# The last image's tail in a two-layer scan kernel: the short scan in the slots' form, its norm and convolution input made inside the output pipeline

## The chip, the cores and the metric

The kernel runs on one core of a Trainium2 chip. The metric is the device time of one execution in microseconds. Five engines work from queues of their own: PE (matrix products into PSUM), DVE (vector work and scans), ACT (activation functions and copies), POOL (element-wise work in SBUF only) and SP (which here issues DMA transfers). They meet through semaphores.

## The reference

Eight images of 64 x 64 positions and 96 channels pass through two layers with residual connections. Each layer is

```python
x = x + layer(group_norm(x))       # 32 groups of 3 channels, over all positions
# layer:
xz = x @ in_proj                   # 96 -> 2 * 192 channels: a value and a gate z
v = silu(depthwise_conv3x3(value)) # 192 channels
y = sum of four scans over the 4096 positions (by rows, by columns, each both ways)
y = layernorm(y) * silu(z)
out = y @ out_proj                 # 192 -> 96
```

A scan of layer 0 is the usual selective scan, `h = exp(dt * A) * h + dt * B * u`, `y = sum over 16 states of h * C + D * u`, where dt (through a softplus), B and C come from the value by small projections. Layer 1 has one set of weights for the four directions, and its scan is written in closed form:

```python
decay = exp(cumsum(dt * A))                   # along the positions
h = decay * cumsum(dt * B * u / (decay + 1e-12))
y = sum over states of h * C + u * D
```

As the accumulated decay falls far below 1e-12, h goes to zero. So in layer 1 only the first positions of each direction add to y beyond u * D. The kernel computes 160 positions of each direction, and a flag computed on the chip (`worst`) tells whether that was enough; if not, a general path, not run here, redoes layer 1.

## The kernel before

**Layout.** Channels lie on partitions: 96 of them in each of NH = 2 halves, 4096 positions in the free dimension. A scan works on 128 partitions, which are 32 channels (a group; NG = 3 groups in a half) by 4 states; so a full tile needs NS = 4 *sets* to cover 16 states.

**The loop over images.** For each image b, `scan_rows` runs the scan of layer 0 in an order written out by hand (`manual_schedule`): step n issues, for neighbouring sets, the loads of replicated rows, the decay, the scan, the read-out and the summing products. Beside it, other stages placed at given steps compute the convolution of image b - 1's layer 1 and of image b + 1's layer 0. At the end of the scan of image b come the sets of the *short* scan of image b - 1's layer 1. Then `out_phase` runs the output pipeline of both finished maps: 8 chunks of 512 positions from each, 16 stages with fixed lags (load x, mean, centring, squares, variance, roots, scaling, affine, gate, projection, residual sum, store), and a plan by which other work can be put at chosen steps.

**The short scan in the slots' form**, as used for images 0 to 6. Only 160 positions at each of four starts matter, and states with larger rates die sooner: 160, 40, 24 and 16 positions suffice for the four sets of states (`HEADS`). All four sets and four directions are packed side by side into one row of 960 (`HT`) columns, so there is one set per group, six in all. `extend` makes the shorter copies of a row. `short_projection` makes dt's input, B and C; `short_ready` makes, per half (a *job*), softplus of dt (`parts`, `exponential`, `logarithm`, `rounded`, `rounding`, and `total`, which sums four terms by products with the identity), dt * u (`product`), the running sum of dt (`running`, `again`), the smallest products for the flag (`lowest`), and stores the three rows to DRAM (`store`). Its tiles dt0, z0, dtu0 and ln0 have one buffer each, and the running sum reuses dt0. Per set, `fetch` and `replicate_short` load the rows replicated over partitions, `fill` makes the decay, `drive` copies dt * u to PSUM, `gate` applies tanh to the running sum (the closed form's factor decay / (decay + 1e-12), written as half of 1 + tanh), and DVE does the rest:

```python
nc.vector.tensor_tensor(s["buf"], s["group"]["drive"], b, ALU.mult)
nc.vector.scalar_tensor_tensor(buf, s["group"]["cum"], 1.0, buf, ALU.add, ALU.mult)
for d in (slice(0, BLOCK), slice(HT - 1, BLOCK - 1, -1)):
    nc.vector.tensor_tensor_scan(
        buf[:, d], s["decay"][:, d], buf[:, d], 0.0, ALU.mult, ALU.add
    )
```

`read_out` multiplies by C on POOL and `collect` sums the states by products on PE. In the listings of profiles these are L857 (decay), L878 (drive), L872 (tanh), L895, L898 and L903 (DVE), L924 (POOL) and L937 (PE); L505 is the copy of `extend`, L798 that of `lowest`.

**The end** is `finish`, for image 7, which has no following image to run beside. In order: the output pipeline of image 7's layer 0 and image 6's layer 1; then the load of image 7's whole layer-0 output x1 from DRAM into the tile x1T (L1835) and of the convolution's weights (`late_conv`, L150 and L157; L159 multiplies the taps); the group norm from sums that the pipeline took; `conv_second`, which normalizes x1T into the padded map xn (L368) and runs `convolution`; then `scan_head`, a form of the short scan of its own; then the output pipeline of that map alone, and the flag.

`convolution` computes the first half's channels by PE up to row 40 and by ACT and POOL beyond it (L301, L303), the second half's by DVE from projections that PE makes and ACT copies into the padded maps xp (L255, L262, L290, L292), and ends each piece with a Silu on ACT (L294).

`scan_head` works on rows of 640 columns, 160 for each direction, for all states alike. POOL copies the starts (L1199), ACT multiplies the map by the summed D (L1238); rows are replicated over partitions by products with `spread` into PSUM (L1185). Each of the six groups does four sets of four scans on DVE (L1178), with a sigmoid for the factor (L1278), products on DVE and POOL (L1271, L1280, L1282) and the sums into the map (L1295). The order of this part, and of everything in `finish` outside of `out_phase`, follows the scheduler of the language from data dependences; tiles from pools that share memory wait for each other.

Of the kernel before, what the change touches and what calls it, by code (L numbers as in the profile page):

```python
# [17 lines left out]
NH = 2  # L18
# [20 lines left out]
CUTS = slice(0, MM), slice(MM, HN)  # L39
# [6 lines left out]

JOINS = slice(HEAD, 3 * HEAD, 2 * HEAD - 1)
# [6 lines left out]
def two_ss2d_layers(ctx: ExitStack, tc: tile.TileContext, t: dict, out: bass.AP):  # L54
# [300 lines left out]
    def conv_second(x1T, st, xc):  # L355

        rows = T // WW
        with (
            tc.tile_pool(name="conv", bufs=1) as pool,
            tc.tile_pool(name="pmm", bufs=4, space=PSUM) as pmm,  # L360
            tc.tile_pool(name="ptap", bufs=1, space=PSUM) as ptap,
        ):
            bank = lambda name: pmm.tile([P, MM], F32, tag="mm", name=name)
            late_conv(1, pool)
            gm, gr, shift = group_norm(st, bank)
            xn = padded(pool, "xn1")
            for i in range(NT):
                nc.vector.tensor_scalar(  # L368
                    xn[:, 1 + i * rows : 1 + (i + 1) * rows, 1 : 1 + WW],
                    grid(x1T[:, i * T : (i + 1) * T]),  # L370
                    gm,
                    gr,
                    ALU.subtract,
                    ALU.mult,
                )
            tap_bank = lambda name: ptap.tile([P, T], F32, name=name)
            convolution(1, xn, xc, pool, bank, tap_bank, PE_ROWS, rows)
        return gm, gr, shift
# [12 lines left out]
    def scan_parts(b):  # L391
# [20 lines left out]
        if b >= 1:  # L412
            unit = dict(short=True, nth=None, n=HT, b=b - 1)
            units.append(unit)
            for h in range(NH):
                jobs.append(dict(unit=unit, h=h))
                for g in range(NG):
                    group = dict(unit=unit, job=jobs[-1], h=h, g=g)
                    sets.append(dict(unit=unit, group=group, i=0, first=False))
        x_dbl = [dram.tile([2 * ROWS, L], F32, name=f"x_dbl{c}", bufs=2) for c in "rc"]  # L420
        return units, jobs, sets, x_dbl

# [83 lines left out]

    def fetch(s, short, loads):

        if s and s["i"] == 0 and s["unit"]["short"] == short:
            group, n = s["group"], s["unit"]["n"]  # L510
            for c in ("dt", "dtu", "cum") if short else ("dt", "dtu"):
                if c == "cum":
                    rep = loads.tile([P, T], F32, tag="bc_rep", name="cum_rep", bufs=2 * NS + 1)
# [17 lines left out]
    def replicate_short(s, c, loads):  # L531

        if s and s["unit"]["short"] and s["group"]["h"] == 0 and s["group"]["g"] == 0:
            unit = s["unit"]
            rep = loads.tile([P, T], F32, tag="bc_rep", name=f"{c}_rep", bufs=2 * NS + 1)
# [630 lines left out]
    def scan_head(xc, worst):  # L1166

        n, cuts, joins = HN, CUTS, JOINS

        def runs(out, decay, drive):

            for d in (slice(0, 2 * HEAD), slice(n - 1, 2 * HEAD - 1, -1)):
                nc.vector.tensor_tensor_scan(  # L1178
                    out[:, d], decay[:, d], drive[:, d], 0.0, ALU.mult, ALU.add
                )  # L1180

        def product(lhs, src, name, m=P):
            ps = psum.tile([P, T], F32, tag="ps", name=name)
            for at in cuts:
                nc.tensor.matmul(ps[:m, at], lhs, src[:, at], start=True, stop=True)  # L1185
            return ps[:m, :n]

        with tc.tile_pool(name="hpiece", bufs=1) as piece, tc.tile_pool(name="hwork", bufs=NS) as work:

            def spare(name, m=P):  # L1190
                bufs = 2 if name == "gate1" else NS
                return work.tile([P, n], F32, tag=name, name=name, bufs=bufs)[:m, :]

            load_late(piece, "spread")
            xs = [spare("decay1", C) for h in range(NH)]
            for h in range(NH):
                for k, at, src in segments(xc[:, h, :]):
                    dst = xs[h][:, k * HEAD + at.start : k * HEAD + at.stop]
                    nc.gpsimd.tensor_copy(shaped(dst, src), src)  # L1199
            m = R + 2 * N  # L1200
            ps = psum.tile([P, T], F32, tag="ps", name="ps_proj1")
            for at in cuts:
                for h in range(NH):
                    nc.tensor.matmul(
                        ps[:m, at],
                        w["wx1"][:, 0, h, :],
                        xs[h][:, at],
                        start=h == 0,
                        stop=h == NH - 1,
                    )  # L1210
            x_dbl = spare("gate1", m)
            nc.scalar.copy(x_dbl, ps[:m, :n])
            b_rep, c_rep = states_rep(x_dbl, n, piece)
            dt, dtu, cum = (
                piece.tile([C, NH, n], F32, name=f"h_{c}") for c in ("dt", "dtu", "cum")
            )
            z, ln = ([spare(c, C) for h in range(NH)] for c in ("drive1", "decay1"))
            for h in range(NH):
                bias = w["dtb1"][:, 0, h : h + 1]
                ps = product(w["dtw1"][:, 0, h * C : (h + 1) * C], x_dbl[:R, :], "ps_dt1", C)  # L1220
                nc.scalar.activation(dt[:, h, :], ps, AF.Relu, bias=bias)
                nc.scalar.activation(z[h], ps, AF.Abs, bias=bias)
            for h in range(NH):
                nc.scalar.activation(z[h], z[h], AF.Exp, scale=-1.0)
# [764 lines left out]
```

## Time and profile before

| quantity | us |
|---|---|
| median of three runs | 12404.24 (12389.48 to 12425.54) |
| the profiled execution, time | 12404.1 |
| its span | 12402.2 |
| output pipeline of two streams | 114.05 (from 11979.00) |
| gap before the convolution | 13.15 (from 12093.05) |
| convolution of layer 1 | 68.39 (from 12106.20) |
| `scan_head`, preparation | 27.06 (from 12174.59) |
| `scan_head`, six groups | 126.70 (from 12201.65) |
| last output pipeline | 69.25 (from 12328.35) |

The stages' borders are instructions in the timelines: the first PE or DVE work after a stage, the last sum of DVE before it. A row of a timeline gives start and length in us, the engine, the line of the kernel, the operation with its tiles, how many were merged, and in brackets how long the engine had idled and for whom. `PEclk` is the share of full rate that was granted to PE.

### The profile page before, as it was taken

Reading aid. Unit: us, or ns where it says so; the run is one execution under the profiler, and the core shown is the slowest. Engines: PE = TensorE matmul, PEld = TensorE weight load, DVE = VectorE, ACT = ScalarE, POOL = GpSimd, SP = SyncE. Lnnn points to the kernel's source line nnn. Section 1 sums busy time; section 2 is a strip of 40 time slices with the busy share of each in tenths; the row PEclk is TensorE's granted clock in tenths of the full one; section 3 lists DMA queues with packets and bytes.
Section 4 is the critical chain, followed back from the end, with each engine's and each line's share of the span. In section 5 each row is a group of like instructions: output and inputs, shape, how many; then the busy total and the mean of one; then the engine's idle time right before and its main releaser. Section 6 shows DMA issues by size and latency. Waiting matters only on the chain. (4 is left out here: it accounts for less than half of the span.)

```text
span 12402.2 us, 134216 instructions
## 1 busy us (share of the span) xinstructions
PE 9540.3 (77%) x44312; PEld 3022.4 (24%) x44312; DVE 10960.4 (88%) x6870; ACT 9688.3 (78%) x15131; POOL 10508.3 (85%) x4802
## 2 busy tenths in 40 slices
PE   5875578787888778877788777888788887886565
PEld 1221122222222222222222222222222222222122
DVE  6999889996999969999799987999879998899976
ACT  4888778887887868878788787887778877788874
POOL 3999889996999969998699986999879987799974
PEclk8887778888888878888888878887788877887786
DMA  3444344444444444444444454444544445444430
GB/s 96 165 155 156 127 159 161 154 156 152 148 164 160 161 138 164 163 162 147 148 156 158 162 165 135 160 162 161 163 138 153 156 156 158 136 165 160 157 123 23
DMA packets 666561, 1853.80 MB, mean 149 GB/s; under 512 B 184936, under 2 KB 199150, under 8 KB 665757
## 3 DMA queue, kind: packets, MB, share of 16 engines
q1 hardware_dynamic: 658685, 1832.52, 44.6%
q10 hardware_dynamic: 7168, 12.59, 0.3%
q8 instruction: 352, 5.77, 0.2%
q14 instruction: 356, 2.92, 0.1%
HBM read 1533.82 MB, written 311.02 MB: 149 GB/s over the span
## 5 line engine op out<-in xcount | busy, mean ns | idle before, releaser
L924 POOL TENSOR_TENSOR out<-set,c_rep 128x1024 f32<-128x1024 f32 x3114 | 7290.0, 2359 | 884.4 <-PE acc L960 317.8
L908 DVE TENSOR_TENSOR_SCAN set<-decay,state,set 128x1024 f32<-128x1024 f32 x2304 | 5366.3, 2345 | 407.4 <-ACT decay L861 189.6
L861 ACT ACTIVATE decay<-dt_rep,w_a 128x1024 f32<-128x1024 f32 x3072 | 3420.2, 1114 | 335.7 <-DVE set L908 329.8
L895 DVE TENSOR_TENSOR set<-drive,b_rep 128x1024 f32<-128x1024 f32 x2346 | 2811.1, 1198 | 43.1 <-DMA b_rep<-x_dblr 28.2
L1027 PE MATMUL ps_conv<-edged,taps 96*96 96x512 f32 (+1 forms) x4032 | 2476.3, 754 | 54.5 <-DVE dt L787 25.9
L960 PE MATMUL acc<-out,w_gather 128*32 128x256 f32 x24576 | 2274.2, 480 | 8.1 <-POOL out L924 7.7
L908 DVE TENSOR_TENSOR_SCAN set<-decay,set 128x1024 f32<-128x1024 f32 x768 | 1744.4, 2286 | 224.5 <-ACT decay L861 146.6
L885 POOL TENSOR_TENSOR set<-dtu_rep,b_rep 128x1024 f32<-128x1024 f32 x768 | 1810.1, 2357 | 93.9 <-DMA b_rep<-x_dblr 51.6
L951 PE MATMUL acc<-map,w_eye 96*32 96x256 f32 x4608 | 568.5, 575 | 1483.4 <-ACT map L990 1253.5
L990 ACT COPY map<-acc 32x256 f32<-32x256 f32 x3072 | 1470.5, 479 | 45.8 <-PE acc L960 5.6
L960 PEld LDWEIGHTS acc<-out,w_gather 128*32 128x32 f32 x24576 | 781.8, 130 | 1939.5 <-issue 1282.0
L1027 PEld LDWEIGHTS ps_conv<-edged,taps 96*96 96x96 f32 (+1 forms) x4032 | 727.5, 200 | 1405.4 <-issue 1244.3
L919 ACT COPY state<-set 128x1 f32<-128x1 f32 x2304 | 426.1, 185 | 754.3 <-DVE set L908 747.9
L634 PE MATMUL ps_sp<-z,w_eye 96*96 96x512 f32 x960 | 658.2, 774 | 288.8 <-ACT ln L643 244.4
L655 POOL TENSOR_TENSOR dtu<-ln,map 96x1024 f32<-96x1024 f32 x256 | 670.7, 2620 | 237.2 <-DVE ln L651 133.0
L878 ACT COPY drive<-dtu_rep 128x1024 f32<-128x1024 f32 (+1 forms) x810 | 808.0, 997 | 34.7 <-DMA dtu_rep<-dtu_far 30.1
L602 PE MATMUL ps_dt<-x_dbl,w_dtw 7*96 7x512 f32 x1024 | 595.4, 663 | 301.2 <-ACT z L615 151.0
L951 PEld LDWEIGHTS acc<-map,w_eye 96*32 96x32 f32 x4608 | 101.4, 121 | 1954.6 <-ACT map L990 1656.1
L634 PE MATMUL ps_sp<-dtu,w_eye 96*96 96x512 f32 x960 | 554.6, 662 | 0.0
L634 PE MATMUL ps_sp<-ln,w_eye 96*96 96x512 f32 x960 | 535.5, 642 | 0.0
L614 ACT ACTIVATE dt<-ps_dt 96x512 f32<-96x512 f32 x512 | 303.0, 592 | 279.2 <-PE ps_dt L602 260.0
L634 PE MATMUL ps_sp<-dt,w_eye 96*96 96x512 f32 x960 | 506.7, 610 | 0.0
(239 smaller groups left out, 9496.8 us busy)
## 6 DMA issues: line engine op xcount, KB each, us to landing
dt_rep<-dt_far SPq DMA_DIRECT2D x768, 512.0 KB
dtu_rep<-dtu_far SPq DMA_DIRECT2D x768, 512.0 KB
b_rep<-x_dblr SPq DMA_DIRECT2D x256, 512.0 KB
c_rep<-x_dblr SPq DMA_DIRECT2D x256, 512.0 KB
b_rep<-x_dblc SPq DMA_DIRECT2D x256, 512.0 KB
c_rep<-x_dblc SPq DMA_DIRECT2D x256, 512.0 KB
dt_far<-ln SPq DMA_DIRECT2D x256, 384.0 KB
dtu_far<-dtu SPq DMA_DIRECT2D x256, 384.0 KB
```

The costliest lines, as they stand in the source:

```text
L634: nc.tensor.matmul(job["ps"][:C, :], w["eye"], job[term][:, halves[s]], start=i == 0, stop=i == 3,)
L655: nc.gpsimd.tensor_tensor(like(job["dtu"], col), like(job["dt"], col), positions(xc[:, h, :], col, t0, T), ALU.mult,)
L861: nc.scalar.activation(s["decay"], s["group"]["dt"], AF.Exp, scale=rate)
L878: nc.scalar.copy(s["group"]["drive"], s["group"]["dtu"])
L885: nc.gpsimd.tensor_tensor(s["buf"], s["group"]["dtu"], b, ALU.mult)
L895: nc.vector.tensor_tensor(s["buf"], s["group"]["drive"], b, ALU.mult)
L908: nc.vector.tensor_tensor_scan(ordered(s["buf"], unit), ordered(s["decay"], unit), ordered(s["buf"], unit), 0.0 if unit["nth"] == 0 else s ...
L924: nc.gpsimd.tensor_tensor(s["out"], s["buf"], s["unit"]["c", s["i"]], ALU.mult)
L951: nc.tensor.matmul(acc, lhs[:, GC * g : GC * (g + 1)], positions(old[:, h, :], unit["column"], unit["t0"] + at, n), start=True, stop=False ...
L960: nc.tensor.matmul(acc, w["gather"], s["out"][:, at : at + n], start=False, stop=s["i"] == NS - 1, skip_group_check=True,)
L990: nc.scalar.copy(yk, like(acc, unit["column"]))
L1027: nc.tensor.matmul(job["ps"][:C, :], taps[l][:k, h, tap, :], edged[:k, tap // 3 : tap // 3 + rows, tap % 3 : tap % 3 + WW], start=tap == 0 ...
```

## The change

Four things change, all in what follows the scan of image 7.

1. `finish` lets the output pipeline keep the new x in x1T: chunks of x are loaded straight into slices of x1T and the residual sum is written there. It is still stored to DRAM, but no longer loaded back. x1T and a pool `last` with xn and the convolution's weights are allocated on the right side, where the scan's loads were.
2. The group norm's stages are put at steps 19 to 24 of that output pipeline, with one load of ACT's table ahead of the last, and the four pieces of normalization (`stage_second`) at steps 26 to 29. `late_conv` runs before the pipeline.
3. The map of image 6 in that pipeline (y1) takes a buffer of `keep` under the tag "map".
4. `scan_head` and its constants are gone. `scan_last` uses the slots' form: the twelve copies of starts on DVE, `extend`, `short_projection`, `short_ready` for both jobs, the products by the summed D on DVE, then a loop in hand-written order over the six sets. `add_sums` adds each group's sums into the map. The ring of replicated rows has 4 buffers instead of 9.

```diff
+    def stage_second(x1T, xn, i, norm):
+        rows = T // WW
+        at = xn[:, 1 + i * rows : 1 + (i + 1) * rows, 1 : 1 + WW]
+        src = grid(x1T[:, i * T : (i + 1) * T])
+        nc.vector.tensor_scalar(at, src, norm[0], norm[1], ALU.subtract, ALU.mult)

-    def conv_second(x1T, st, xc):
+    def conv_second(x1T, st, xc, staged=None):
...
-            late_conv(1, pool)
-            gm, gr, shift = group_norm(st, bank)
-            xn = padded(pool, "xn1")
...
+            if staged:
+                xn, norm = staged
+            else:
+                late_conv(1, pool)
+                norm = group_norm(st, bank)
+                xn = padded(pool, "xn1")
+                for i in range(NT):
+                    stage_second(x1T, xn, i, norm)

-                    rep = loads.tile([P, T], F32, tag="bc_rep", name="cum_rep", bufs=2 * NS + 1)
+                    rep = loads.tile([P, T], F32, tag="bc_rep", name="cum_rep", bufs=ring(s))

-    def scan_head(xc, worst):
...
+    def scan_last(b, xc):
+        unit, jobs, sets = short_parts(b)
+        unit["ring"] = 4
+        with (
+            tc.tile_pool(name="piece", bufs=1) as piece,
+            tc.tile_pool(name="loads", bufs=2) as loads,
+            tc.tile_pool(name="work", bufs=2) as work,
+        ):
+            xs[b] = piece.tile([C, NH, HT], F32, name="x_short")
+            for h in range(NH):
+                for k, at, src in segments(xc[:, h, :]):
+                    dst = xs[b][:, h, place(0, k)][:, at]
+                    nc.vector.tensor_copy(shaped(dst, src), src)
+                extend(xs[b][:, h, :])
+            with tc.tile_pool(name="pmisc", bufs=4, space=PSUM) as pmisc:
+                for _, stage in short_projection(xc, None, unit, piece, pmisc):
+                    stage()
+                for job in jobs:
+                    for _, stage in short_ready(xc, None, job, piece, pmisc):
+                        stage()
                 for h in range(NH):
...
+                    for i in range(NT):
+                        at = xc[:, h, i * T : (i + 1) * T]
+                        nc.vector.tensor_scalar(
+                            at, at, w["dsum1"][:, h : h + 1], None, ALU.mult
+                        )
...
+                for n in range(-4, len(sets) + 4):
+                    at = lambda i: sets[n + i] if 0 <= n + i < len(sets) else None
+                    replicate_short(at(AHEAD_BC), "b", loads)
+                    fetch(at(2), True, loads)
+                    replicate_short(at(AHEAD_BC - 1), "c", loads)
+                    advance_set(at(0), None, work)
+                    fill(at(1), pslot)
+                    drive(at(1), True, pdrive)
+                    gate(at(1))
+                    read_out(at(-1), work)
+                    collect(at(-2), xc, xc, pacc)
+                    add_sums(at(-3), xc)
+
+    def add_sums(s, y):
+        if not s:
+            return
+        h, g = s["group"]["h"], s["group"]["g"]
+        for k, at, dst in segments(y[GC * g : GC * (g + 1), h, :]):
+            part = shaped(s["group"]["acc"][GC * k : GC * (k + 1), at], dst)
+            nc.vector.scalar_tensor_tensor(dst, part, 0.5, dst, ALU.mult, ALU.add)

     def finish(b, y):
...
-        with tc.tile_pool(name="x1T", bufs=1) as pool1:
+        with tc.tile_pool(name="x1T", bufs=1, side="right") as pool1:
             x1T = pool1.tile([C, L], F32, name="x1T")
-            nc.sync.dma_start(x1T, x1[b])
-            xc = keep.tile([C, NH, L], F32, name="map")
-            norm = conv_second(x1T, st, xc)
-            with rotating():
-                scan_head(xc, worst)
+            with tc.tile_pool(name="last", bufs=1, side="right") as last:
+                late_conv(1, last)
+                xn = padded(last, "xn1")
+                with tc.tile_pool(name="behind", bufs=1) as pool:
+                    plan, put = planner()
+                    def chunk(i, _):
+                        x = x1T[:, i * MM : (i + 1) * MM]
+                        nc.sync.dma_start(x, t["x"][b][:, i * MM : (i + 1) * MM])
+                        return x
+                    first = list(finish_first(b, y, st, pool))
+                    first[3] = chunk
+                    streams = [tuple(first)]
+                    if b >= 1:
+                        streams.append(second_of(b - 1, keep, pool, pool, put))
+                    def beside(pmm):
+                        bank = lambda name: pmm.tile([P, MM], F32, tag="mm", name=name)
+                        stages, found[1] = group_norm_stages(st, bank)
+                        put(24, nc.scalar.preload_act_table_set, "natural_log_exp_and_others")
+                        for step, stage in zip((19, 20, 21, 22, 23, 24), stages, strict=True):
+                            put(step, stage)
+                        for i in range(NT):
+                            put(26 + i, lambda i: stage_second(x1T, xn, i, [found[1]["gm"], found[1]["r"]]), i)
+                        return plan
+                    out_phase(*streams, plan=beside)
+                norm = tuple(found[1][x] for x in ("gm", "r", "shift"))
+                xc = keep.tile([C, NH, L], F32, name="map")
+                conv_second(x1T, st, xc, (xn, norm))
+            scan_last(b, xc)
             out_phase(finish_second(norm, xc, kept(x1T), out[b]))
```

## The prediction

> **What bounds the kernel now.** The change touches only what follows the scan of the last image, so I first asked the view of windows for the busy time of each engine in the last stages of the span (columns: window, length, then busy us and instructions of PE, PEld, DVE, ACT, POOL, then clock, DMA share, GB/s).
>
> ```profile
> 11979.00:12093.05 114.05, 104.70 (x247) 33.15 (x242) 70.10 (x83) 88.80 (x122) 78.75 (x48) 1.00 0.35 91
> 12093.05:12106.20 13.15, 0.00 (x1) 0.03 (x1) 0.91 (x2) 0.58 (x2) 1.17 (x11) 0.54 0.74 172
> 12106.20:12174.59 68.39, 51.12 (x114) 18.92 (x114) 49.52 (x40) 29.76 (x32) 28.34 (x11) 0.87 0.00 0
> 12174.59:12201.65 27.06, 13.67 (x26) 5.71 (x27) 11.76 (x18) 22.43 (x25) 7.41 (x18) 0.56 0.32 107
> 12201.65:12328.35 126.70, 56.05 (x255) 22.78 (x253) 104.14 (x121) 48.76 (x54) 66.94 (x56) 0.50 0.01 3
> 12328.35:12397.60 69.25, 63.27 (x118) 18.09 (x118) 31.69 (x32) 38.59 (x50) 38.70 (x24) 0.82 0.07 21
> ```
>
> In order these are the output pipeline of two streams (PE bound), a gap in which every engine is idle and only the DMA works, the convolution of layer 1, the preparation of `scan_head`, its six groups, and the last output pipeline. Together they are 3.4% of the span. The groups are the largest part and DVE leads them (104.14 of 126.70). The timeline of DVE shows one group, 21.07 us from 12226.63 to 12247.70, in series with POOL, ACT and PE:
>
> ```profile
> 12226.63 5.54 DVE L1178 TENSOR_TENSOR_SCAN drive<-decay,drive 128x320 f32<-128x320 f32 x4
> ...
> 12242.11 0.65 DVE L1295 TENSOR_TENSOR map<-acc,map 32x160 f32<-32x160 f32 x2 [2.26 <-PE acc L1285]
> ...
> 12246.77 0.83 DVE L1280 TENSOR_TENSOR drive<-drive,gate 128x640 f32<-128x640 f32 x1 [1.23 <-ACT gate L1278]
> ```
>
> The same work in the slots' form exists in this trace: the six sets of image 6, which close the scan of image 7.
>
> ```profile
> 11948.78 2.20 DVE L903 TENSOR_TENSOR_SCAN set<-decay,set 128x480 f32<-128x480 f32 x2
> 11950.90 1.13 DVE L895 TENSOR_TENSOR set<-drive,b_rep 128x960 f32<-128x960 f32 x1
> 11952.12 2.26 DVE L898 SCALAR_TENSOR_TENSOR set<-cum_rep,set 128x960 f32<-128x960 f32 x1
> 11954.42 2.20 DVE L903 TENSOR_TENSOR_SCAN set<-decay,set 128x480 f32<-128x480 f32 x2
> ```
>
> There DVE is busy without a break and a set takes 5.64 us (11948.78 to 11954.42). The waits of DVE and POOL name the gap:
>
> ```profile
> DVE xn L368 <- DMA w_cw<-in_cw: 12.2, 1, 12.2
> ...
> 12095.70 0.22 POOL L231 MEMSET xn<- 96x66 f32 x1 [5.69 <-DMA out<-x_in]
> ```
>
> The small load is only the last of a batch behind the 1.5 MB load of x1T issued at 12095.63; that one is what is late.
>
> **Part 1: norm and convolution input.** Removed: x1T's load and its wait. x now stays in x1T, loaded by chunks that take the place of the x_in loads one for one; the sums of the norm are taken as before. DVE normalizes the first of four pieces (0.75 us, 2.98 for four) right after its last sum at 12093.05; the norm's ten small ACT instructions are issued before that (ending about 12091.8, one table load less), so PE can project at 12093.9 instead of 12106.20. But the padded maps of the convolution lie where the output chunks lay, so POOL's memsets and ACT's first copy still wait for the last output store: 12095.7, against 12108.27 now. With PE warm, three copies at 0.56 put DVE's first tap at 12097.4 against 12110.61: 13.2 us. Against it: the tap product (1.05 us) and its four loads move to the head of the output pipeline. On SP the loads stand before ys_far's second store and wait for POOL's last reading of c_rep (ends 11975.9); SP is idle from 11973.3 to 11979.5, and four issues of 0.45 fit. The tap data should land by 11982, and the product sits behind DVE's first centring (11982.12 to 11983.35), where two more centrings and then 2.36 us of idling follow; ACT's third square waits for PE anyway until 11986.9. I charge 0.2 us; landing later costs microsecond for microsecond, since ps_mean, squares and roots queue behind it. y1 takes a map buffer of `keep`; its first load moves ahead into the scan on SP, behind the last store of deltas, which already waited for the last reader of that map. Sum: **-13** (bounds -11 and -14).
>
> **Part 2: preparation.** Zero is the end of the last Silu (12174.59 now); the present kernel needs 27.06 us to its first group. The new one runs two jobs, one per half of the channels, on single buffers (dt0, z0, dtu0, ln0), and ACT holds both jobs ahead of the first set. The second job's first activation overwrites dt0, so it waits until cum has been stored to DRAM. Working:
> - 12 copies on DVE (as on POOL now, 3.15 us together, eight of them before the last Silu ends) and ACT's extensions (0.15 us each in a row, L505): 3.2. They leave POOL.
> - four projections of 480 columns, two ACT copies of 0.55: at 7.6.
> - job 1: first argument, four activations of 0.6, table load 1.28, exp 1.0, load 1.28, ln 1.0, two roundings 1.9: at 16.6. Six products that wait for the roundings: 6.4, at 23.0. Copy 0.56, two scans 0.8: at 25.2. Six extensions 0.9; the store of cum is issued by 26.7, behind two others on SP. The eight small `last_short` (1.6) run beside it.
> - the DRAM write: now x_dbl_far is issued at 12181.27 and its reader at 12184.76, 3.5 us for 97 KB. I take 3.5 (bounds 3 and 6): job 2 starts at 30.2.
> - job 2: 19.6 on the same rows: at 49.8. Then a table load 1.28, the first set's decay 1.95, drive 0.94 and tanh 2.0 (L857, L878, L872): 56.0. The other DRAM trips (b, c, first replicas) end long before.
>
> The eight products by dsum go from ACT to DVE (0.75 each, 6 us) and hide in DVE's idle time while the jobs run on ACT.
>
> **A rule on the tables.** Row: the last activation before L1224 ends at 12186.05, the load takes 1.28 and exp starts at once.
>
> ```profile
> 12186.07 1.28 ACT L1224 ACT_TABLE_LOAD   x1
> 12187.36 1.36 ACT L1224 ACTIVATE drive<-drive 96x640 f32<-96x640 f32 x2
> ```
>
> [...] The row shows no drain: I add nothing.
>
> **A rule on the clock.** PE is idle before each burst, so it starts at half rate, where 480 columns take about 1.6 us instead of 0.8.
>
> ```profile
> 12180.00:12184.00 4.00, 2.71 (x7) 1.18 (x8) 0.00 (x0) 4.00 (x6) 0.00 (x0) 0.84 0.06 20
> ...
> 12348.00:12352.00 4.00, 4.00 (x5) 1.07 (x6) 1.91 (x2) 2.53 (x4) 1.71 (x2) 0.50 0.00 0
> 12352.00:12356.00 4.00, 4.00 (x8) 1.05 (x7) 3.09 (x3) 3.44 (x5) 1.26 (x1) 0.83 0.00 0
> ```
>
> [...] With the rule the chain is the 56.0 above; with these rows the projection and both bursts of six stay at half rate, about 9.3 us more, 65.3. I take 58.6, nearer to the rule because the burst nearest in kind (12175) followed it.
>
> **Part 3: six sets.** From the first tanh: gate product 1.16 and scans 2.20; three more sets, the first at 5.2 and then 5.64; then per set the six sums of `add_sums` (six now take 1.75, L1295) also run on DVE, but POOL's product (2.21) ends beneath them, so that the gate product is back at 1.16 instead of 2.26: 6.2 for sets five and six. Then four rounds of sums, 7. Sum: 3.4 + 16.5 + 12.4 + 7 = 39.3. ACT needs 4.9 per set and hides. Replicas: each set's three loads (480 KB each) wait on SP for buffers freed two sets earlier; the DMA moved up to 418 GB/s here, so 1.47 MB take about 4 us and hide beneath 5.6. A set then costs that only if landing exceeds about 7 us.
>
> So scan_last takes 58.6 + 39.3 = 98 against 27.06 + 126.70 = 153.8 now: **-56**. The last output pipeline is unchanged (69.25). The reduction of `least_all` that falls away is one of the rows of 0.2 us at the start. Total -13 - 56 = -69 on the profiled execution, 12404.1 us (span 12402.2), which equals the median (12404.24): **12336 us**, -0.55%. What this measurement can tell from no change is about 0.3%, 37 us.
>
> **Rivals.**
> - *The serial preparation eats half.* Each DRAM write takes 6, PE stays at half rate, ACT's small dependent instructions take 0.28 each in full (they do alone) instead of 0.2: 65.3 + 2.5 + about 8, preparation 75. Gain 13 + 40: 12352; with the tap load late as well, 12365. For it: nothing runs beside the chain to hide any of it. Against: the rows above.
> - *Clock and start are kinder.* PE warms in every burst and again 4 us into the last pipeline instead of after 20 (about -8), and ACT starts the convolution's terms a microsecond earlier; with the 2.6 charged above for half rate: 12324.
> - *Slower.* The replicas bind: in this trace they were primed beside the long scan; here bc_rep has 4 buffers instead of 9, and set n's cum waits for set n-2's gate product. If issue to landing took 20 us or more a set, six sets would cost 120 + 58.6 + 7 = 186 against 153.8, less 13: 12423. It is slower from about 17 us a set on. Against: dt_rep was issued at 11944.16 and ACT used it at 11946.88.
> - *It doesn't do what it says*: the norm is held by the output stores, so part 1 gives 10 instead of 13: inside the range.
>
> **How the numbers follow.** Forecast 0.72 (own range 12320 to 12355), serial preparation 0.14, kinder clock 0.11, replicas 0.03. Beyond 37 us faster lie the forecast, the kinder clock and a bit more than half of the second: 0.91; same 0.06, slower 0.03. The range takes in both clock cases and most of the second rival, and the 36 us between the shown runs: 12308 to 12372.
>
> **What would show it.** In the profile after: the idle gap before the convolution 2 to 4 us instead of 13; from the last Silu to the first 128x960 gate product 55 to 65 us with ACT waiting some 3 us for a store before job 2; sets at 5.6 and 6.2; 95 to 105 us to the last sum. Wrong if ACT waits for dt_rep or DVE for cum_rep by more than a microsecond a set, if the output pipeline exceeds 115, or if preparation exceeds 75.

## The result, and the profile after

The changed kernel took 12348.95 us (median of five, 12318.57 to 12370.30) beside 12415.04 for the kernel before: a ratio of 0.9952, 95% interval 0.9936 to 0.9968, so 40 to 79 us less (the recorded ratio puts the gain at 60 us, the two medians at 66). Timed again on another occasion (e9 below) the ratio was 0.9956 (0.9941 to 0.9971).

Stage by stage, in the two profiled executions (12404.1 us before, 12341.47 us after, span 12339.6). Here the pipeline is counted from DVE's first centring to the end of its last sum, the convolution from its first tap to the end of the last Silu:

| stage | before, us | after, us | difference |
|---|---|---|---|
| up to the first centring behind the scan of image 7 | 11982.12 | 11972.27 | -9.9 |
| output pipeline of two streams | 110.93 | 121.65 | +10.7 |
| last sum to the convolution's first tap | 17.57 | 3.57 | -14.0 |
| convolution | 63.98 | 63.34 | -0.6 |
| short scan (last Silu to last sum) | 153.55 | 100.19 | -53.4 |
| last output pipeline | 69.47 | 73.93 | +4.5 |
| rest | 4.62 | 4.63 | 0.0 |

The first row can't be laid to the change. In further traces of the same two kernels it reads 11995.84 (before, e8), 11998.82 and 11980.63 (after, e1 and e9). So it is by luck that it nearly cancels the 10.7 us of the second row in this pair.

The same stages in the view of windows of the kernel after (pipeline, gap, convolution, preparation, sets, last pipeline; columns as in the prediction):

```profile
11969.15:12093.24 124.09, 117.05 (x251) 35.92 (x248) 68.50 (x83) 88.68 (x122) 78.73 (x48) 0.89 0.30 80
12093.24:12094.80 1.56, 0.00 (x1) 0.03 (x1) 1.56 (x3) 0.00 (x0) 0.00 (x0) 1.00 0.05 18
12094.80:12160.84 66.04, 48.72 (x114) 18.17 (x114) 49.46 (x46) 29.68 (x33) 28.61 (x15) 0.91 0.01 3
12160.84:12219.67 58.83, 32.71 (x52) 10.27 (x52) 11.15 (x24) 33.75 (x77) 4.99 (x16) 0.65 0.37 115
12219.67:12261.03 41.36, 17.02 (x192) 14.19 (x192) 38.55 (x59) 23.17 (x45) 13.28 (x6) 0.66 0.42 139
12261.03:12334.96 73.93, 67.67 (x118) 19.09 (x118) 31.78 (x32) 38.62 (x50) 38.72 (x24) 0.77 0.07 20
```

The gap of 13.15 us is down to 1.56. The groups' 126.70 us have become 41.36, in which DVE is busy for 38.55. Preparation has grown from 27.06 to 58.83, as foreseen. What was not foreseen stands in the clock column: 0.89 in the first line where it was 1.00, 0.77 in the last where it was 0.82.

The start of the convolution, in the timelines of DVE and POOL:

```profile
12093.24 0.69 DVE L1579 TENSOR_TENSOR x_in<-ps_out,x_in 96x512 f32<-96x512 f32 x1 [2.11 <-PE ps_out L1494]
12093.85 2.97 DVE L357 TENSOR_SCALAR xn<-x1T,gn_gm,gn_r 96x1024 f32<-96x1024 f32 x4
12097.50 1.34 DVE L287 TENSOR_SCALAR ps_tap<-xp,w_cw,w_cb 96x1024 f32<-96x1024 f32 x1 [0.68 <-POOL xp L230]
...
12096.40 0.58 POOL L228 MEMSET xp<- 96x66 f32 x1 [5.35 <-DVE xn L357]
```

The norm begins as the last sum ends, and the first tap follows 3.6 us after that sum; POOL's memsets of the padded maps, held until 12096.40, are the last thing that it waits for. The memset's row names DVE, whose third piece of xn ends at 12096.10; but the last output store, issued at 12093.96, landed at 12096.01 in the trace, and the waits of POOL and ACT for it end within 0.03 us of that.

Preparation, in ACT's timeline (job 1, the wait, job 2, the first set):

```profile
12170.39 1.28 ACT L752 ACT_TABLE_LOAD   x1
12171.68 1.00 ACT L752 ACTIVATE z<-z 96x960 f32<-96x960 f32 x1
...
12175.92 1.00 ACT L759 ACTIVATE dtu<-dtu 96x960 f32<-96x960 f32 x1
12182.13 0.56 ACT L777 COPY ln<-ps_sp 96x480 f32<-96x480 f32 x1 [5.21 <-PE ps_sp L768]
12184.94 0.56 ACT L777 COPY ln<-ps_sp 96x480 f32<-96x480 f32 x1 [2.26 <-PE ps_sp L768]
...
12193.34 0.66 ACT L748 ACTIVATE dt<-ps_dt,w_dtb 96x480 f32<-96x480 f32 x1 [4.42 <-DMA cum_short<-dt]
...
12213.56 1.28 ACT L865 ACT_TABLE_LOAD   x1
```

Job 2's first activation waits 4.42 us for the store of the running sum. The gaps of 5.21 and 2.26 us are PE's sums, the first at half rate, the second at full rate. The table load of 1.28 us starts 0.02 us after the activation before it ends, and exp starts 0.01 us after the load: no drain, that is no idle time between them, here either.

The sets, in DVE's timeline (the second, and the turn to the fifth):

```profile
12224.35 2.02 DVE L906 SCALAR_TENSOR_TENSOR set<-cum_rep,set 128x960 f32<-128x960 f32 x1 [0.23 <-ACT cum_rep L880]
12226.41 2.20 DVE L911 TENSOR_TENSOR_SCAN set<-decay,set 128x480 f32<-128x480 f32 x2
12228.53 1.13 DVE L903 TENSOR_TENSOR set<-drive,b_rep 128x960 f32<-128x960 f32 x1
12229.75 2.17 DVE L906 SCALAR_TENSOR_TENSOR set<-cum_rep,set 128x960 f32<-128x960 f32 x1
...
12239.61 1.73 DVE L1227 SCALAR_TENSOR_TENSOR map<-acc,map 32x160 f32<-32x160 f32 x6
12241.37 1.16 DVE L903 TENSOR_TENSOR set<-drive,b_rep 128x960 f32<-128x960 f32 x1
12242.62 1.16 DVE L906 SCALAR_TENSOR_TENSOR set<-cum_rep,set 128x960 f32<-128x960 f32 x1
...
12257.51 3.52 DVE L1227 SCALAR_TENSOR_TENSOR map<-acc,map 32x160 f32<-32x160 f32 x12 [1.46 <-PE acc L945]
```

From scan to scan a set takes 5.5 us, later 6.3 to 6.5 with its sums, and the gate product is 1.16 us long again once POOL's product lies beneath the sums. No set waits for a replica; the wait of 0.23 is for tanh.

### The profile page after: what moved, and what is told of

Same layout as the page of the kernel before. It is cut to its first block, busy times and chain, and to the rows that moved or that the text cites. A ratio compares the mean times of both kernels' runs of the same rounds, so it can differ in the third digit from the quotient of the medians.

```text
span 12339.6 us, 134054 instructions
## 1 busy us (share of the span) xinstructions
PE 9488.0 (77%) x44276; PEld 3013.1 (24%) x44276; DVE 10889.7 (88%) x6819; ACT 9677.8 (78%) x15172; POOL 10439.8 (85%) x4748
## 5 line engine op out<-in xcount | busy, mean ns | idle before, releaser
L1035 PE MATMUL ps_conv<-edged,taps 96*96 96x512 f32 (+1 forms) x4032 | 2435.7, 743 | 54.7 <-ACT z L623 26.3
```

What stands on the lines that cost most here:

```text
L1035: nc.tensor.matmul(job["ps"][:C, :], taps[l][:k, h, tap, :], edged[:k, tap // 3 : tap // 3 + rows, tap % 3 : tap % 3 + WW], start=tap == 0 ...
```

## The experiments

Single executions of one kernel differ by up to 60 us (12375 to 12435 for the kernel before), so what follows is read from the stages of each trace. The question was first where the 10.7 us in the pipeline came from, then what the parts give alone, then what is left in preparation and in the last pipeline.

**Again: the changed kernel (e1), the kernel before (e8), and the changed kernel timed (e9).** No edit.

> The changed kernel once more, for a second trace of it. The output pipeline of two streams took 121.7 us from its first centring to the last sum in the first trace of it, against 110.9 before. Theory A: PE fell to half rate at the head of the pipeline (11978 to 12001) by the chance of where windows of 3.41 us fall, in which PE's work is counted; then this trace may show about 111 with PE at full rate there, or about 121 with the same fall, and the tap product costs nothing. Theory B: the work moved to the head of the pipeline (four loads, the tap product, x loaded into x1T) costs 10 us itself; then 120 or more again, whatever PE's rate. The rest as in the first trace: scan_last about 100 us from the last Silu to the last sum.

> The kernel before once more, for a second trace of it. Theory A (where the clock's windows fall is chance from run to run): the pipeline may show half rate at its head and 121 to 123 us here too. Theory B (part 1 brings it about): 110.9 again, with no half rate. Its time says how far two executions of one kernel differ: 12375 to 12428 so far.

> The changed kernel, timed beside the two that follow. Theory A: its time is that of before less 53 (scan_last), less 14 (start of the convolution), plus 4.4 (the last pipeline's longer stretch at half rate), whatever the pipeline's 111 or 122 by chance in either: about -63, a ratio near 0.995. Its trace shows 111 or 121 to 123 us for the pipeline of two streams, by the columns that PE counts in the window that opens 0 to 3 us after the first centring (half rate below some 2000 of 4096, full rate above).

Measured: the second trace of the changed kernel showed 121.64 us again, and PE at half rate for 27.3 us. That looked like theory B. But the second trace of the kernel *before* (e8) showed 121.50 with the same 27.3, and the third of the changed kernel (e9) 110.99 with none. The fall in e8:

```profile
11997.97:12001.39 3.42, 2.01 (x5) 0.38 (x4) 1.56 (x2) 1.99 (x3) 3.16 (x3) 1.00 0.95 245
12001.39:12004.80 3.41, 3.41 (x8) 0.90 (x6) 1.22 (x1) 0.30 (x1) 3.41 (x4) 0.50 1.16 233
```

Theory A stands: like for like the two kernels differ by 0.1 us (121.50 and 121.65, 110.93 and 110.99).

Why it falls can be read from the trace when the windows are cut where the granted clock changes. All changes lie on one grid of 3.413 us. In the first trace after:

```profile
11971.14:11974.55 3.41, 3.10 (x6) 0.72 (x6) 2.28 (x3) 1.03 (x1) 2.43 (x2) 1.00 0.62 195
11974.55:11977.97 3.42, 2.00 (x5) 0.38 (x4) 2.21 (x2) 1.99 (x3) 3.31 (x3) 1.00 0.56 137
11977.97:11981.38 3.41, 3.12 (x7) 0.90 (x6) 1.22 (x1) 0.41 (x3) 3.41 (x4) 0.50 0.87 231
...
11998.45:12001.86 3.41, 3.41 (x5) 1.14 (x4) 2.24 (x2) 0.19 (x1) 2.77 (x3) 0.50 0.00 0
12001.86:12005.27 3.41, 3.41 (x8) 0.87 (x7) 0.56 (x1) 3.06 (x4) 0.00 (x0) 1.00 0.00 0
```

and in e9, of the same kernel:

```profile
11983.35:11986.77 3.42, 2.14 (x4) 0.38 (x4) 1.83 (x3) 2.11 (x2) 3.42 (x4) 1.00 0.69 148
11986.77:11990.18 3.41, 3.05 (x10) 0.93 (x10) 1.62 (x2) 1.46 (x3) 3.41 (x3) 1.00 0.98 263
```

The second line of the first fence is the cause: PE is busy for only 2.00 us of that window, since it waits 1.24 us for POOL's sum of squares, and the next window is at half rate. In e9 the same wait lies 0.44 us otherwise within its window, PE is busy for 2.14 us, and the rate stays. PE's instructions are the same in both. Adding up the columns that PE's records stream in a window (a product of 512 columns makes two records; in the trace after one starts every 0.85 us at half rate, so that four, 2048 columns, fit in, and every 0.43 us at full rate, about eight, 4096 columns) gives, for the window that decides at the pipeline's head:

| trace | columns | pipeline, us | half rate in all of it, us |
|---|---|---|---|
| before | 2042 | 110.9 | 0 |
| before, again (e8) | 1839 | 121.5 | 27.3 |
| after | 1859 | 121.6 | 27.3 |
| after, again (e1) | 1853 | 121.6 | 27.3 |
| after, timed (e9) | 2048 | 111.0 | 0 |
| part 1 alone (e2) | 1709 | 123.0 | 34.1 |
| part 2 alone (e3) | 2024 | 110.9 | 0 |
| two dt0 (e4) | 1725 | 123.0 | 34.1 |
| taps late (e5) | 1857 | 118.3 | 20.5 |
| both jobs (e7) | 2048 | 111.0 | 0 |

In each trace that fell, one window (3.4 us) of the last column lies near the pipeline's end and the rest at its head. In e2 and e4 the deciding window opens before the first centring, in the others 1.9 to 2.7 us after it.

In this table the border lies between 1859 and 2024 columns, about half of what fits. It is about the same count on the way back, and that is what makes the fall dear: at half rate only 2048 columns fit into a window, so PE gets its rate back only after a window almost without a gap. In the pipelines and the convolution of all fourteen traces, windows of up to 1996 columns at half rate were followed by another, and those of 2034 and more ended it; but four with less (1798 to 1987) ended it too. At full rate, two windows (1808 and 1991) kept the rate and two (1997 and 2077) lost it against the border.

Most of these exceptions hold products of 128 rows, where the others have 96. When a column of 128 rows is counted as 1.33 columns of 96, one border at about 2020 fits both directions, and of 1057 windows two are left over: one of 1987 that ended half rate, one of 2077 that lost full rate. So columns alone are not what counts; rows count too, and "half of what fits" holds for products of 96 rows.

Luck at the head was partly paid for later, in both traces with part 1 and no added products that kept full rate there (e9 and e7). In e9 the window before the convolution counted 1932 columns, and PE fell there:

```profile
12088.96:12092.58 3.62, 2.02 (x5) 0.67 (x6) 1.65 (x3) 0.75 (x4) 0.00 (x0) 1.00 0.22 66
12092.58:12095.99 3.41, 3.41 (x5) 1.13 (x6) 1.93 (x3) 0.58 (x1) 1.07 (x7) 0.50 0.16 48
```

The first tap came after 5.20 us instead of 3.57, the convolution took 66.77 instead of 63.34 and the short scan 102.80 instead of 100.19: 7.7 of the 10.7 us were gone again (in e7 the first two read 5.22 and 66.74). From the first centring to the last sum of all, e9 took 359.7 us, after 362.7 and e1 362.6; before 415.5 and e8 425.1.

**Part 1 alone (e2) and part 2 alone (e3).** In e2 the old short scan follows part 1; in e3 the new one follows the old `finish`.

```diff
-            scan_last(b, xc)            # e2; e3 is the reverse, in the finish of before
+            with rotating():
+                scan_head(xc, worst)
```

> Only part 1: x kept in x1T, norm and input of the convolution in the pipeline, with the old scan_head behind it. Forecast's terms: from the last sum of the pipeline to the first tap of DVE 3.6 us instead of 17.6 (-14), scan_head unchanged at 153.5, so 12390 beside the 12404 of before. If theory B holds the pipeline gives 10 of the 14 back (first centring to last sum 121); if A holds it does so only where PE falls to half rate at its head.

> Only part 2: the short scan of the last image in the slots' form, with the old pipeline, the load of x1T and the norm behind it. Forecast's term: from the last Silu to the last sum 100 us instead of 153.5 (-53), so 12350. Theory B: the pipeline of two streams, which has no tap product here, stays at 111 us. Theory A: 111 or 121 by chance. Rival for the gain itself: if it hung on memory that part 1 frees, scan_last would take over 105 here.

Measured: part 1 alone brought the last sum and the first tap to 3.59 us of each other, with the short scan at 153.14. Part 2 alone brought the short scan to 100.01, with that gap at 17.65. So each part gives its own gain and needs nothing of the other. The pipeline took 123.02 and 110.88, by the columns of the table. The last pipeline took 69.57 with the old scan before it and 73.90 with the new one.

**The taps off the pipeline's head (e5).**

```diff
-                late_conv(1, last)
-                xn = padded(last, "xn1")
...
+                        put(12, late_conv, 1, last, lambda product: put(18, product))
+                        put(14, lambda: found.update(xn=padded(last, "xn1")))
```

> The changed kernel with the convolution's loads, the zeroing of xn's border and the tap product taken from the head of the output pipeline and put at its steps 12, 14 and 18. All four traces with part 1 had PE at half rate for 27 or 34 us at the pipeline's head and took 121.6 to 123.0 us from the first centring to the last sum; both without part 1 had none of it and took 110.9. Theory B: these moved instructions bring it about: then 111 here. Theory A: they do not; where the windows of the clock fall does, which comes out of the scan before: then 121 to 123 again, or 111 only if the window that opens 2 to 3 us after the first centring counts over 2000 columns.

Measured: half rate for 20.5 us and 118.3 us, with 1857 columns in the window at issue. By itself this excludes only that the loads, memsets and tap product at the head are needed for the fall; together with e8, the kernel before that falls without any of part 1, it frees them. The length of the stretch varies too: here a window of 2034 columns ended it two windows earlier than in the first trace after.

**PE kept busy in both pipelines (e6).**

```diff
+                    if burst is not None and k == 0 and burst:
+                        idle(pvar, "ps_var", burst)        # burst = 8 ahead of the last pipeline
+                    if burst is not None and 2 <= k <= 6:
+                        idle(pz, "ps_z", 1)
```

> The changed kernel with products that nobody reads on PE: one of 512 columns at each of steps 2 to 6 of both last output pipelines, and eight ahead of the last one, in time in which PE idles. Theory (clock): what lengthens both pipelines is PE at half rate, which it enters where a window counts less than about half of its columns and leaves only after one without a gap; then the pipeline of two streams takes about 111 us instead of 121.6 to 123.0 with no half rate at its head, and the last one about 63 instead of 73.9. Rival: half rate is not what binds there (ACT's and POOL's squares and sums are); then both stay within 2 us, or grow by the products' own 0.5 us each.

Measured: the pipeline of two streams 112.41, with no half rate (1.4 us above the 111 of the unaided traces at full rate); the last one 65.43 instead of 73.9, with 3.4 us of half rate instead of 34.1. The first 30.7 us of the last pipeline, e6 first, then after:

```profile
12259.29:12290.00 30.71, 30.00 (x70) 8.92 (x69) 14.58 (x14) 18.81 (x24) 21.98 (x17) 1.00 0.00 0
```
```profile
12261.03:12291.70 30.67, 28.43 (x34) 6.33 (x35) 11.10 (x10) 12.95 (x15) 17.89 (x15) 0.50 0.00 1
```

In the same time PE gets through 70 records instead of 34 (some of them the added ones), ACT through 24 instead of 15. Half rate was what bound there, and the rival falls; the forecast of 63 was 2.4 us too good. Which of the thirteen products does it, the eight ahead or the five between, was not separated.

**Two buffers for dt0 (e4).** `tile_of("dt0")` gets `bufs=2` in `scan_last`.

> The changed kernel with two buffers for dt0, so that the second job's first activation no longer waits for the store of the first job's running sum. Theory: that wait (4.4 us of ACT ahead of job 2 in the trace after) is a plain addition to the chain; job 2 starts about 28 us after the last Silu instead of 32.5 and scan_last takes about 96 instead of 100.2. Rival: the stores of dt and dtu, issued half a microsecond earlier, are what job 2 meets next (its logarithm overwrites ln0, its rounding dtu0), and the wait only moves there: then 100 again with 3 to 4 us of waiting at the logarithm.

Measured: job 2 starts 28.0 us after the last Silu instead of 32.5, without any wait, in ACT's timeline:

```profile
12189.48 1.41 ACT L807 ACTIVATE last_short<-dt,least 96x2 f32<-96x2 f32 x7
12190.80 0.64 ACT L749 ACTIVATE dt<-ps_dt,w_dtb 96x480 f32<-96x480 f32 x1
```

The logarithm does not wait for its store either. The short scan takes 96.46 us, 3.7 less: most of the 4.42 us of the wait was a plain addition to the chain.

**Both jobs side by side (e7).** Besides the lines shown, all four tiles of a job get two buffers, and `set` and `out` two instead of their four.

```diff
-                for job in jobs:
-                    for _, stage in short_ready(xc, None, job, piece, pmisc):
-                        stage()
+                steps = [at for job in jobs for at in short_ready(xc, None, job, piece, pmisc)]
+                for _, stage in sorted(steps, key=lambda at: at[0]):
+                    stage()
```

> The changed kernel with two buffers of dt0, z0, dtu0 and ln0 in scan_last (and two instead of four of set and out, to make room), and the stages of the two jobs issued step by step side by side: two table loads fewer, no wait for a store ahead of job 2, one job's products beside the other's activations. Theory: preparation is a serial chain and the second job's 20 us lie on it in full; here scan_last takes about 85 us instead of 100.2 (first sets about 43 us after the last Silu instead of 58.8). Rival: the chain is bound by ACT's own work (some 30 us for both jobs) and PE's sixteen products at half rate; then it gives 6 or less, 94 and more.

Measured: 98.81 us, the rival's side. Two table loads and the wait are gone, but PE's sums of both jobs now come in one run that starts at half rate, and all stores come at its end: the first set's decay starts 52.1 us after the last Silu instead of 54.0. PE's timeline, and below it the row of ACT's that waits for the first replica:

```profile
12195.45 6.71 PE L768 MATMUL ps_sp<-z,w_eye 96*96 96x480 f32 x8 [3.61 <-ACT z L752]
12202.24 1.91 PE L768 MATMUL ps_sp<-dtu,w_eye 96*96 96x480 f32 x2
...
12209.76 0.97 PE L768 MATMUL ps_sp<-dt,w_eye 96*96 96x480 f32 x2
...
12228.59 1.28 ACT L865 ACT_TABLE_LOAD   x1 [7.49 <-DMA dt_rep<-dt_short]
```

In the rows of PE a sum (two records) starts every 1.6 to 1.7 us at half rate, later every 0.8. In this trace PE was at half rate when preparation began, as in e9, where the short scan took 102.80; against that one e7 gained 4.0.

**Warm sums (e11), on top of the two dt0 and the warm pipelines (e10).**

```diff
+            if s == 1 and "deep" in unit:
+                job["v"] = bank(s, "ps_fill")
+                for _ in range(8):
+                    src = job["dt"][:, halves[1]]
+                    nc.tensor.matmul(job["v"], w["eye"], src, start=True, stop=True)
```

> The changed kernel with two buffers for dt0 and with the products that keep PE at full rate in both last output pipelines. From the single parts: scan_last 96.4 instead of 100.2, the pipeline of two streams 112 in every run instead of 111 or 122, the last one 65.4 instead of 73.9: 13 us less than the changed kernel where its pipeline kept full rate, 23 less where it did not. If the parts don't add up, because the last pipeline starts from another phase of the clock, it keeps some half rate there: then 5 to 9 less.

> As the kernel with two dt0 and warm pipelines, with eight products of 480 columns more in each job of scan_last, right after the job's four activations, while PE waits for exp and ln, read by nobody. Theory: PE's sums (six products that wait for the roundings) start at half rate and take 8 us with the two before them; warmed by a window without a gap they take about 4, in both jobs: scan_last about 88 to 90 us instead of 96.4. Rival: the eight products themselves (6.4 us at half rate) end later than the roundings and push the sums, or the window is cold again by then: no gain, 95 or more.

Measured, e11: 0.9942 (0.9926 to 0.9958), 12335.38 us beside 12417.22 before. The short scan took 99.74 us, which is more than the 96.46 of e4 without them. PE's timeline:

```profile
12163.79 9.72 PE L755 MATMUL ps_fill<-dt,w_eye 96*96 96x480 f32 x16 [1.04 <-ACT dt L749]
12173.34 0.97 PE L774 MATMUL ps_sp<-z,w_eye 96*96 96x480 f32 x2
12174.15 0.97 PE L774 MATMUL ps_sp<-dtu,w_eye 96*96 96x480 f32 x2
```

They did warm PE: a sum starts every 0.8 us from the first on. But they last until 12173.3, 2.5 us after the roundings are done, and the sums of z, which before ran during the roundings, now stand behind them. All eight sums end 25.3 us after the last Silu instead of 24.1. The rival was right.

Measured, e10: 0.9922 (0.9902 to 0.9942), 12324.38 us beside 12417.22 before and 12355.67 for the changed kernel on the same chip. Its stages: pipeline 114.13 (the forecast was 112 in every run; here one window near its end was at half rate), last pipeline 63.73, but the short scan 101.50 instead of 96.4: its projection ended 7.4 us after the last Silu, as in e9, instead of 6.2, since PE was at half rate longer there. The chain from the first centring to the last sum took 348.0 us, 11.7 less than e9 and 14.7 less than after.

**Four more products behind the last projection (e12), on top of e10.**

```diff
+                    if burst == 0 and n + 10 <= k < n + 12:
+                        idle(pz, "ps_z", 2)
```

> The kernel with two dt0 and warm pipelines, and four more products of 512 columns that nobody reads behind the last projection of the pipeline of two streams, where PE waits for xn. In the traces whose last window before the convolution counted 1907 to 1936 columns of 4096, PE fell to half rate there, the first tap came 4.9 to 5.2 us after the last sum instead of 3.6 and the convolution and preparation took 3 to 8 us longer; where it counted 2048 they did not. Theory (clock): with the four products that window counts 2500 or more in any phase: 3.6 us to the first tap, convolution 63.4, scan_last 96.5, pipeline 112 to 114, last pipeline 64 to 65.5, so 341 to 344 us from the first centring to the last sum, and a time some 85 below before. Rival: the four products end after xn is there and push the convolution by up to 1 us, and preparation starts from another phase: 345 and more.

Measured: 0.9937 (0.9924 to 0.9951), 12325.76 us beside 12406.70: 81 us less than before. Convolution 63.41, short scan 95.54, pipelines 114.13 and 65.42; 343.65 us from the first centring to the last sum, 16 less than e9 and 19 less than after. Between the last sum and the first tap PE keeps its rate, yet the first tap still comes 5.15 us after the last sum. PE's timeline, and the row of DVE's first tap:

```profile
12077.53 3.60 PE L1567 MATMUL ps_z<-taps,w_eye 96*96 96x512 f32 x8
12080.96 5.93 PE L252 MATMUL ps_in<-xn,w_in 96*96 96x512 f32 x15
12083.56 1.34 DVE L287 TENSOR_SCALAR ps_tap<-xp,w_cw,w_cb 96x1024 f32<-96x1024 f32 x1 [2.25 <-ACT xp L259]
```

The first piece of xn is there at 12079.1, but the four products hold PE until 12081: the convolution's projections begin 2.54 us after the last sum instead of 0.87 in the trace after, and the first tap waits for ACT's copies of them. These 1.7 us cover the whole delay of 1.6. The rival was right on the kind of it, but allowed 1 us; the theory's total (341 to 344) came all the same.

So e10 and e12 beat both kernels: by their medians 31 us against the changed kernel (e10, same chip), by the traces 12 to 19.

## Why the prediction was right, and where it was not

- **Total.** Forecast -69 us, measured -66 between the medians (-62 with e9), interval -40 to -79. 12348.95 lies inside the range and 13 us above the forecast, 11 of them because the kernel before came out at 12415.04 instead of the 12404.24 that the forecast started from.
- **Part 1, -13.** Right: -14.0 in the traces after, e1 and alike in e2, the idle gap 1.56 us (-12.4 in e9, where PE had fallen to half rate). The bound named, POOL's memsets behind the output store, is the one in the timeline (the store landed at 12096.01). The charge of 0.2 us for the tap product was right too: like for like the pipelines differ by 0.1.
- **Part 2, preparation: 58.6 us forecast, 58.8 measured** from the last Silu to the first gate product. The sum is better than its terms. The start was cheaper (x_dbl copied at 6.8 us instead of 7.6). From there to the store of cum job 1 took 21.1 against 19.1. The round trip to DRAM took 4.58 us from the issue of the store to job 2, against 3.5 taken (bounds 3 and 6); job 2 took 20.2 against 19.6, and the rest 6.1 against 6.2. The 2.6 us that the forecast charged for half rate thus paid for 1.1 us of the round trip too; agreement to 0.2 us is partly luck.
- **Sets: 39.3 forecast, 41.4 measured.** The first four sets came as forecast (20.0 us to the end of the fourth scan, against 19.9), sets five and six took 12.8 against 12.4. Too small was the term of 7 us for the last rounds of sums: 8.6 us from the end of the last scan, 1.46 of it a wait for PE's sums.
- **The rows on table loads and on the clock.** In the trace after a table load took 1.28 us, with 0.02 us between it and the activation before and 0.01 us between it and exp: the forecast rightly added nothing. On the clock its 58.6 us leaned to 56.0, a chain in which PE soon has its full rate in each burst; no run shows that term. In its place the runs showed a rate that changes on the grid of 3.413 us, by the columns of the window before. In the trace before, the burst of 12175.05 had full rate from 12179.3 on, the last pipeline only from 12353.4 on, 25 us after its start. In the trace after, the six sums had full rate again 5.8 us after their start in job 1 and 4.4 us in job 2, and took 7.9 and 7.2 us against 6.4 in the forecast; PE was at half rate for 37 of the first 54 us of preparation. The length of preparation came out all the same, partly by luck, as said above.
- **"The last output pipeline is unchanged": wrong.** It takes 73.9 to 74.1 us in six of the seven traces that run the new short scan unaided by added products (72.5 in the seventh) and 69.5 to 69.6 in the three that run the old one. The prediction had seen the 20 us at half rate in it and carried them over as a constant; they are 34 us now instead of 25, and e6 shows that they are what costs. The term left out is +4.4 us. Why the windows lie so consistently worse behind the new scan stays open.
- **"Wrong if the output pipeline exceeds 115": it did,** 121.65, and the reason was none of those weighed. The step that failed is to read one trace's pipeline at full rate (1.00 in its first line) as a property of the kernel. e8 and e9 show that either kernel has both lengths.
- **Rivals.** Replicas never bound. The "serial preparation" priced at 75 us did not come. The "kinder clock" was the opposite of what happened in the last pipeline, though its mechanism, PE's rate there, was the right place to look, and as an edit (e6) it is worth the 8 us named.

What repeats from trace to trace is -14.0 (start of the convolution), -53.1 (short scan, means of three and three traces in like phases) and +4.4 (last pipeline), together -63; what does not is where the clock's windows fall, up to 10 us in the whole tail.

## What to carry to other kernels

Before a stage length is taken from one trace as "unchanged", look at the granted clock in it: where PE's work in a window of 3.4 us is close to the border (here about 2000 of 4096 columns, for products of 96 rows), the same instructions give two lengths (here 110.9 and 121.6 us), and only like phases may be compared. A stage that PE bounds and enters at half rate can stay there because it has small gaps (17 to 34 us on end in the pipelines here); thirteen idle products ahead of it and in its first steps, in time that PE has anyway, were worth 8 us here, while idle products that end after real operands are ready only moved the delay. Packing work for the width of an engine (six sets of 5.5 us for six groups of 21) repaid a preparation twice as long, and the one buffer that tied a job to a store cost most of the wait that ACT's row showed (3.7 of 4.4 us).

## What the runs showed of the hardware that was not expected

- In these traces the granted clock changes only on a grid of 3.413 us. About 2000 columns of 96 rows in a window are the border in both directions: with fewer at full rate (1709 to 1936 in the windows at the pipelines' heads and last sums) the next window was at half rate, and only a window as good as full (2034 and more of 2048, with one exception once rows are counted) ended it. PE stayed at half rate for 17 to 34 us on end in a pipeline while its timeline showed it busy nearly without a break.
- Two executions of one kernel fell on nearly the same phase of that grid (pipelines of 121.65 and 121.64 us, with starts 26.5 us apart), a third on another. What ties the phase to the program was not tried.
- From the issue of a store of 360 KB, the third of three in 0.9 us, to the start of what waited for it: 4.58 us.
